# A graph-attention and a graph-convolution layer: q's row through ScalarE's queue, pads in disjoint rows, one full product for the fifth sum, and a new order

## The chip, the cores and the metric

The kernel runs on one core of a Trainium2 chip. The time is the device time of one execution in microseconds (us); several executions are made, and their median is the figure. Everything is computed in float32.

Engines are named as in the profile: PE is TensorE's matmul side, PEld its loading of stationary operands, DVE is VectorE, ACT is ScalarE, POOL is GpSimd and SP is SyncE, which here only issues DMAs. ACT and POOL can issue DMAs too, each on a queue of its own.

## The reference

Two layers work on 32 batches of a 512 x 1024 matrix x (512 channels c, 1024 nodes n). `adj` is 512 x 512, `wq` and `wk` have 512 entries.

```python
# layer 0
h = jnp.maximum(_layernorm(x, axis=-1), 0.0)
q = jnp.einsum('c,bcn->bn', wq, h)
k = jnp.einsum('c,bcn->bn', wk, h)
scores = q[:, None, :] + k[:, :, None]
scores = jnp.where(scores > 0, scores, 0.01 * scores)
att = jax.nn.softmax(scores, axis=-1)
agg = jnp.einsum('bcn,bmn->bcm', h, att)
x = x + jax.nn.relu(jnp.einsum('oc,bcm->bom', adj, agg) + bm[None, :, None])
# layer 1
h = jnp.maximum(_layernorm(x, axis=-1), 0.0)
x = x + jnp.einsum('bnf,nm->bmf', h, adj * adj) + bias
```

The attention of node m depends on q[n] + k[m] alone, with one slope where the sum is positive and another where it is not. The kernel therefore never builds the 1024 x 1024 scores. It sorts the nodes by q, multiplies first (adj times h gives a value vector of 512 for every node), and forms running sums of exp(q) times value from one end of the sorted order and of exp(0.01 q) times value from the other. A node m then needs one row of each sum, picked by the rank of -k[m] among the q.

## The kernel before

For each batch the work is cut into small steps, each a Python function. The names are those of the plan.

- `load` brings the four tiles of x (128 channels x 1024 nodes each, 512 KB). `stats`, `norm`, `slopes` and `relu` make h of them.
- `scores` multiplies h by wq and wk on PE (tile `pq`), copies the result to `qr` on ACT, writes q's 1024 numbers to a DRAM tile `qd` (4 KB) on SP's queue, and reads them back on the same queue, broadcast to 128 partitions, as `qrow` (512 KB). The read waits for the write. `columns` transposes `qr` for q and k by partitions (`qk`). `factors` takes the maximum of q.
- `rank` counts on DVE, for each of 8 blocks of 128 nodes, how many q are smaller. `to_rows` turns four blocks' counts into row indices. `lower` counts on ACT, with Sign, for k; `from_rows` makes indices of that.
- `value` (PE, 8 products of 4 x 128 channels into a PSUM bank each) and `spread` (ACT, PSUM to SBUF) make the value rows; `scatter` writes them on POOL's queue, by index, to their sorted places in a DRAM table `td`. Five tables are used in turn.
- `fetch` reads the sorted table back in three tiles `vs` of three blocks each. There are NB = 9 blocks of 126 nodes, and each block has 2 x 64 rows. All scatters of the batch must have landed. The pool of these tiles has five buffers, so the third tile of a batch waits until sums 3 to 5 of the batch before are through with theirs.
- `weights` takes exponentials of the q column of the fetched rows. `later` adds the identity's columns (`wc`). `stationary` multiplies two 128 x 64 masks by three blocks' weights on POOL (`sm`). `totals` sums the denominators.
- `scan` makes the i-th running sum on PE: two products of 64 columns each, one per direction, for blocks 8 - i and i, into the two halves of one PSUM bank `sc`. `sums` carries the last row of each half into the next blocks (ACT, 1 x 512 copies), copies the bank out and stores it to `td` on SP. So scan i + 1 waits for `sums` i.
- `gather` picks three rows for each node by index on POOL's queue; `excess`, `divide`, `weigh` (ACT) and `combine` (DVE) join them; `turn` transposes on PE and adds to x.
- `reload`, `lift` and the second set of statistics lead to layer 1: `propagate` (PE, 8 pieces of 4 products) and `finish`, which issues the store of the result.

Once, at the start, `adjacency` loads adj, `turn_adjacency` transposes it (16 transposes on PE, four copies on ACT), `square` squares it on POOL, `masks` builds the masks, `biases` loads the bias. `pads` fills the places of the five tables that no node takes: for both directions the first row of every block and all 64 rows of the last block. It issues twenty DMAs from SP.

The order is written out as times. `PLAN` holds a due time for every step, relative to its batch; batch b is moved by b times `T` (80.54). `FIRST` and `LAST` hold a shift and a stretch for the first and last five batches. All steps of all batches are sorted by due time and issued in that order; each engine then runs its own instructions in that order, and waits where data are missing. The times are used for sorting only.

Where two DMAs of SP or ACT share one of eight completion semaphores, the later one also waits for the earlier one.

Of the kernel before, what the change touches and what calls it, by code (L numbers as in the profile page):

```python
# [9 lines left out]
F32 = mybir.dt.float32  # L10
# [6 lines left out]
P = 128  # L17
# [5 lines left out]
QUAD = 32  # L23
# [4 lines left out]
    "adjacency": (-101.07,),  # L28
    "biases": (44.64,),
    "columns": (4.2,),  # L30
    "combine": (
        294.87, 297.97, 299.08, 299.37, 299.3, 299.78, 294.64, 298.25, 297.13,
        300.21, 294.04, 296.69, 302.3, 302.51, 299.3, 302.5,
    ),
    "compare_mask": (-67.81,),
    "divide": (278.8,),
    "excess": (273.86,),
    "factors": (28.62,),
    "fetch": (75.46,),
    "finish": (355.71, 359.91, 377.15, 379.07, 388.37, 416.37, 407.17, 420.62),  # L40
    "from_rows": (83.21,),
    "gather": (249.25, 252.21, 260.07, 256.74, 257.75, 255.56, 251.6, 251.28),
    "later": (83.88,),
    "lift": (346.92, 351.32, 359.81, 351.92),
    "load": (-124.99, -84.4, -100.42, -56.07),
    "lower": (25.57, 12.42, 17.04, 27.8, 11.25, 13.48, 43.56, 47.47),
    "masks": (4.76,),
    "norm0": (-21.98,),
    "norm1": (325.76,),
    "pads": (32.59,),  # L50
    "propagate": (350.28, 351.24, 354.2, 368.59, 377.8, 385.91, 388.55, 393.68),
    "rank": (17.09, 15.7, 21, 21.66, 25, 25.14, 23.99, 25.66),
    "reload": (283.74, 288.13, 272.56, 292.92),
    "relu0": (-11.86, -11.33, -11.17, -11.16),
    "relu1": (334.17, 334.3, 335.44, 339.75),
    "scan": (90.31, 96.47, 108.29, 124.9, 142.06, 153.31, 174.19, 187.88, 206.23),
    "scatter": (46.2, 50.63, 47.64, 43.66, 56.05, 51.39, 52.63, 55.96),
    "scores": (-0.21,),
    "slopes0": (-17.18,),
    "slopes1": (327.63,),  # L60
    "spread": (10.74, 18.48, 13.48, 5.99, 31.17, 24.35, 24.62, 20.5),
    "square": (63.05,),
    "stationary": (83.89, 118.42, 168.32),
    "stats0": (-75.55, -62.59, -67.51, -40.04),
    "stats1": (318.33, 318.56, 319.25, 319.54),
    "sums": (91.26, 100.33, 117.83, 130.05, 147.14, 161.48, 177.9, 193.73, 222.2),
    "to_rows": (25.72, 29.81),
    "totals": (89.77,),
    "turn0": (308.02, 308.31, 307.91, 309.59),
    "turn1": (311.69, 310.85, 311.38, 312),  # L70
    "turn_adjacency": (-8.51,),
    "value": (5.59, 16.27, 4.02, 0.51, 21.28, 16.92, 17.52, 16.87),
    "weigh": (286.06, 287.71, 288.75, 285.95, 287.8, 285.85, 291.87, 291.57),
    "weights": (82.11,),
}
FIRST = {
    "columns": ((11.5, 0), (-7.65, 0), (-3.08, 0), (-4.96, 0), (0.81, 0)),
    "combine": ((11.98, -0.904), (3.93, 0.084), (-0.42, 0.777), (-2.07, 1.063), (3.77, -0.867)),
    "divide": ((-1.51, 0), (4.23, 0), (4.06, 0), (-1.38, 0), (-4.23, 0)),
    "excess": ((2.66, 0), (2.27, 0), (2.29, 0), (3.01, 0), (0.22, 0)),  # L80
    "factors": ((41.36, 0), (40.19, 0), (17.96, 0), (6.13, 0), (12.19, 0)),
    "fetch": ((-6.64, 0), (1.09, 0), (-2.72, 0), (-0.25, 0), (1.04, 0)),
    "finish": ((-0.92, -0.273), (0.38, -0.374), (9.14, 0.111), (-2.55, -0.545), (-1.59, -0.253)),
    "from_rows": ((-13.03, 0), (112.54, 0), (-18.02, 0), (5.07, 0), (43.09, 0)),
    "gather": ((11.61, 0.221), (11.9, -0.839), (7.76, 0.785), (2.8, -0.886), (-0.43, 0.506)),
    "later": ((2.05, 0), (-0.44, 0), (-0.72, 0), (-1.2, 0), (1.78, 0)),
    "lift": ((-3.95, -0.084), (-2.84, -0.648), (17.86, 0.674), (18.88, 0.507), (6.94, 0.337)),
    "load": ((-22.66, 0.032), (-29.56, -0.171), (-16.88, 0.669), (-52.23, 0.939), (-3.3, 0.266)),
    "lower": ((13.95, -0.331), (-5.6, -0.741), (-7.9, -0.46), (7.69, -0.008), (6.58, -0.474)),
    "norm0": ((-17.56, 0), (-16.62, 0), (-4.18, 0), (-1.3, 0), (6.51, 0)),  # L90
    "norm1": ((1.78, 0), (0.29, 0), (-1.09, 0), (0.44, 0), (12.94, 0)),
    "propagate": ((-0.94, -0.576), (-0.21, -0.368), (3.5, -0.199), (5.67, -0.457), (-4.69, -0.221)),
    "rank": ((11.44, 0.484), (9.25, -0.392), (3.13, 1.029), (0.87, -0.157), (3.38, -0.145)),
    "reload": ((-8.27, -0.219), (-0.04, 0.298), (7.54, -0.347), (3.32, -0.281), (9.62, 1.296)),
    "relu0": ((-3.11, -0.86), (0.49, 0.979), (-3.24, 0.727), (-0.45, -0.352), (5.51, -0.464)),
    "relu1": ((2.99, 0.363), (6.63, -0.187), (5.31, -0.95), (8.3, 0.53), (10.39, -0.443)),
    "scan": ((-3.42, -0.009), (-0.72, 0.032), (-3.2, -0.075), (-2.89, -0.005), (-0.35, -0.002)),
    "scatter": ((10.77, 0.257), (-0.73, -0.181), (-11.52, 0.027), (16.18, -0.191), (8.18, 0.362)),
    "scores": ((-3.29, 0), (-9.38, 0), (-3.01, 0), (-4.84, 0), (-2.22, 0)),
    "slopes0": ((-19.05, 0), (4.68, 0), (-8.01, 0), (0.99, 0), (10.12, 0)),  # L100
    "slopes1": ((0.11, 0), (2.69, 0), (11.33, 0), (8.09, 0), (12.97, 0)),
    "spread": ((25.99, 0.616), (4.65, 0.327), (6.4, -0.418), (8.18, -0.066), (2.31, 0.757)),
    "stationary": ((0.59, -0.046), (3.58, 0.024), (-1.58, -0.061), (-4.74, -0.096), (2.23, -0.014)),
    "stats0": ((-18.91, 0.792), (-26.56, 0.18), (-12.87, 0.716), (-14.05, 0.414), (-0.39, 0.587)),
    "stats1": ((1.74, 0.57), (2, -0.774), (-1.08, 0.928), (3.45, -0.808), (5.73, 0.388)),
    "sums": ((-1.76, -0.009), (-1.55, -0.001), (-1.11, -0.098), (-1.11, 0.005), (-0.91, -0.007)),
    "to_rows": ((12.57, 0.861), (6.07, -0.299), (4.35, -0.554), (16.06, 0.147), (-0.33, -0.011)),
    "totals": ((-0.61, 0), (-0.11, 0), (-0.4, 0), (-1.59, 0), (-2.46, 0)),
    "turn0": ((9.6, 0.239), (0.12, 1.463), (3.72, -0.389), (2.48, 1.014), (11.58, 0.097)),
    "turn1": ((5.85, 1.247), (7.03, 0.695), (0.1, -0.107), (-2.36, -0.153), (1.12, 1.09)),  # L110
    "value": ((17.29, 0.126), (-1.93, 0.747), (-1.01, 0.425), (-2.88, 0.246), (-2.48, 0.124)),
    "weigh": ((1.61, 0.137), (0.7, -0.519), (2.4, 0.126), (-4.71, 0.923), (-4.76, -0.192)),
    "weights": ((-3.08, 0), (-0.37, 0), (-0.37, 0), (-1.7, 0), (1.43, 0)),
}
LAST = {
    "columns": ((-7.28, 0), (0.79, 0), (-4.33, 0), (2.89, 0), (0.4, 0)),
    "combine": ((75.93, 0.626), (15.35, -0.941), (5.15, 0.497), (6.86, 0.364), (11.64, -0.543)),
    "divide": ((63.12, 0), (25.51, 0), (3.63, 0), (-8.62, 0), (22.62, 0)),
    "excess": ((28.91, 0), (14.61, 0), (-1.25, 0), (-10, 0), (23.88, 0)),
    "factors": ((-15.6, 0), (18.35, 0), (-16.21, 0), (1.83, 0), (-4.13, 0)),  # L120
    "fetch": ((5.65, 0), (-2.32, 0), (-2.42, 0), (-1.37, 0), (0.79, 0)),
    "finish": ((295.78, -0.788), (84.93, 0.121), (31.35, 0.185), (13.03, 0.342), (8.47, -0.005)),
    "from_rows": ((14.61, 0), (-17.87, 0), (24.1, 0), (-4.82, 0), (-22.08, 0)),
    "gather": ((21.35, -0.228), (-4.99, 0.169), (-6.2, 0.647), (-0.69, 0.387), (24.11, 0.85)),
    "later": ((5.5, 0), (1.61, 0), (-5.88, 0), (-2.68, 0), (0.1, 0)),
    "lift": ((309.49, -0.684), (24.34, 0.156), (8.09, -0.277), (-12.65, 0.02), (0.77, 0.013)),
    "load": ((6.11, 0.011), (-7.3, 0.306), (-3.56, 0.076), (1.31, -0.245), (-2.7, 0.142)),
    "lower": ((25.31, -0.108), (4.14, -0.215), (9.69, -0.156), (2.83, -0.069), (-13.68, -0.57)),
    "norm0": ((-13.5, 0), (-4.32, 0), (-12.1, 0), (0.42, 0), (3.16, 0)),
    "norm1": ((254.22, 0), (9.35, 0), (11.35, 0), (-0.46, 0), (6.61, 0)),  # L130
    "propagate": ((281.75, -0.768), (77.94, 0.675), (26.01, 0.587), (18.85, 0.574), (12.12, 0.012)),
    "rank": ((-6.82, -0.047), (-0.18, 0.987), (3.76, -0.308), (-4.68, -0.157), (-9.98, -0.199)),
    "reload": ((91.8, -0.567), (16.08, -0.302), (4.34, 0.859), (-4.18, 0.357), (-6.61, -0.681)),
    "relu0": ((2.55, -0.699), (0.68, 0.648), (5.21, 0.81), (-0.38, 0.398), (6.21, 0.601)),
# [23 lines left out]
def kernel(  # L158
# [357 lines left out]
    def stationary(s, i):  # L516
# [7 lines left out]
        for n in range(3):  # L524
            s.sm[i + n] = [m[:, k, n, :] for k in range(2)]
# [160 lines left out]
```

## Time and profile before

| | us |
|---|---|
| median of 3 runs | 2416.62 |
| lowest and highest | 2409.54 and 2420.97 |
| profiled execution | 2409.72 |
| span of the profile | 2408.0 |

| engine | busy us | share of the span |
|---|---|---|
| PE | 2307.4 | 96% |
| DVE | 1941.3 | 81% |
| ACT | 1585.4 | 66% |
| POOL | 724.6 | 30% |

The span runs from the first to the last instruction; the execution takes 1.7 us more. The mean granted clock of PE is 0.981 of full speed. An engine's busy time does not say what sets the end: the kernel has a start in which data are missing, a long middle in which every batch looks alike, and an end. They have to be read apart, by stretches of time. In a timeline a row shows the start, the duration, the engine, the line, the operation and its tiles, and in brackets the idle time before it with what ended it. A float32 product appears as two passes, so each PE row counts twice as many instructions as the code has products. The DMA queue of SP appears as SPq, and the time of a DMA there is that of its issue, not of its transfer.

### The profile page before, as it was taken

What the parts mean: (1) busy time and instruction counts of PE and PEld (TensorE: products, weight loads), DVE (VectorE), ACT (ScalarE), POOL (GpSimd) and SP (SyncE); (2) the same over time, 40 slices, a digit from 0 to 9 for tenths busy, and PEclk for the clock granted to TensorE, in tenths of its full rate; (3) what the DMA queues carried; (4) which work ended last, traced back from release to release, by engine and by line L of the source; (5) the groups of instructions that cost most, each with busy time, mean ns of one, the idle gap of its engine ahead of it and who ended that gap; (6) DMA issues with size and microseconds to landing.
All of it is one profiled execution on the core that took longest, in us unless ns stands there. A gap on an engine that the chain in (4) does not pass through costs nothing.

```text
span 2408.0 us, 28425 instructions
## 1 busy us (share of the span) xinstructions
PE 2307.4 (96%) x7632; PEld 1004.8 (42%) x7632; DVE 1941.3 (81%) x5008; ACT 1585.4 (66%) x2880; POOL 724.6 (30%) x973
## 2 busy tenths in 40 slices
PE   6787899999999999999999999999999999999797
PEld 3233344444444444444444444444444444444343
DVE  6448788888888888888888888888898888788675
ACT  4566667667766766777676777676677776677541
POOL 2213332323342232333233233323323313323210
PEclk9898999999999999999999999999999999999899
DMA  4678889988889988988898988898898888888972
GB/s 160 184 184 273 267 264 299 279 265 279 307 262 295 299 262 260 303 290 277 290 285 246 298 295 284 270 309 255 270 304 289 268 294 250 262 268 268 284 290 101
DMA packets 206916, 643.49 MB, mean 267 GB/s; under 512 B 29130, under 2 KB 29258, under 8 KB 206756
## 3 DMA queue, kind: packets, MB, share of 16 engines
q1 hardware_dynamic: 147828, 372.67, 54.1%
q0 software_dynamic: 57344, 268.99, 30.2%
q8 instruction: 62, 1.02, 0.2%
q14 instruction: 98, 0.80, 0.1%
q10 hardware_dynamic: 1584, 0.01, 0.0%
HBM read 429.94 MB, written 211.62 MB: 266 GB/s over the span
## 4 chain that ended last, share of the span: by engine, by line
PE 86%; DMA 6%; DVE 3%; ACT 2%; issue 1%; SPq 1%; POOL 1%; POOLq 0%; DVEq 0%; ACTq 0%
PE pg L595 34%; PE pv L447 33%; PE sc L530 12%; PE tr L588 4%; DMA vs<-td 3%; PE pq L344 2%; DVE g L581 1%; DMA td<-pad 1%; DMA g<-td,idg 1%; DVE junk L389 0%; DMA out_dram<-y 0%; DMA x<-in_x_dram 0%; ACT junk L400 0%; DMA qd<-qr 0%; POOL g L552 0%
## 5 line engine op out<-in xcount | busy, mean ns | idle before, releaser
L595 PE MATMUL pg<-h,wsq 128*128 128x512 f32 x2048 | 912.7, 598 | 11.1 <-ACT h L332 11.1
L447 PE MATMUL pv<-wmT,x 128*128 128x512 f32 x2048 | 909.5, 599 | 5.6 <-ACT x L332 5.6
L595 PEld LDWEIGHTS pg<-h,wsq 128*128 128x128 f32 x2048 | 378.7, 190 | 510.0 <-issue 468.5
L447 PEld LDWEIGHTS pv<-wmT,x 128*128 128x128 f32 x2048 | 383.3, 191 | 498.7 <-issue 439.3
L520 POOL TENSOR_TENSOR sm<-mask_a,wc 128x192 f32<-128x192 f32 x96 | 49.9, 519 | 1289.4 <-DVE wc L497 830.9
L530 PE MATMUL sc<-vs,sm 128*64 128x512 f32 x1152 | 324.2, 631 | 60.0 <-POOL sm L520 39.2
L581 DVE SCALAR_TENSOR_TENSOR g<-g,cf 128x512 f32<-128x512 f32 x512 | 347.8, 746 | 12.4 <-ACT g L577 12.4
L460 POOL DMA_INDIRECT td<-v,idx x256 | 293.7, 1147 | 148.8 <-POOL v L459 50.7
L400 ACT ACTIVATE junk<-qrow,qk 128x1024 bf16<-128x1024 f32 x256 | 294.3, 1150 | 4.9 <-DMA qrow<-qd 3.1
L552 POOL DMA_INDIRECT g<-td,idg x256 | 242.9, 949 | 143.6 <-issue 71.6
L540 ACT COPY vs<-sc 1x512 f32<-1x512 f32 x256 | 145.4, 568 | 171.3 <-PE sc L530 171.1
L590 DVE SCALAR_TENSOR_TENSOR y<-tr,nbm,y 128x512 f32<-128x512 f32 x256 | 174.2, 743 | 95.4 <-PE tr L588 89.1
L543 ACT COPY t<-sc 128x512 f32<-128x512 f32 x288 | 168.0, 583 | 94.4 <-DMA td<-t 89.4
L603 DVE SCALAR_TENSOR_TENSOR y<-pg,bm_sb,y 128x512 f32<-128x512 f32 x256 | 187.9, 738 | 42.6 <-PE pg L595 42.3
L389 DVE TENSOR_SCALAR_CACHE_REDUCE junk<-qrow,qk,cnt 128x896 bf16<-128x896 f32 (+6 forms) x224 | 180.4, 805 | 8.2
L530 PEld LDWEIGHTS sc<-vs,sm 128*64 128x64 f32 x1152 | 77.8, 139 | 253.6 <-issue 91.3
L314 DVE BATCH_NORM_STATS2 st<-x 128x6 f32<-128x512 f32 x256 | 162.9, 678 | 25.0 <-DMA x<-in_x_dram 25.0
L384 DVE TENSOR_SCALAR_CACHE_REDUCE junk<-qrow,qk 128x128 bf16<-128x128 f32 (+6 forms) x224 | 165.5, 739 | 13.6 <-DMA qrow<-qd 8.8
L577 ACT ACTIVATE g<-g,cf 128x512 f32<-128x512 f32 x256 | 163.5, 711 | 7.4 <-DVE cf L571 7.4
L338 DVE TENSOR_TENSOR y<-y,bias_sb 128x1024 f32<-128x1024 f32 x128 | 155.1, 1230 | 8.4 <-ACT h L332 8.4
L314 DVE BATCH_NORM_STATS2 st<-y 128x6 f32<-128x512 f32 x256 | 159.1, 663 | 0.0
L454 ACT COPY v<-pv 128x512 f32<-128x512 f32 x256 | 142.2, 580 | 21.6 <-PE pv L447 17.8
(109 smaller groups left out, 1939.0 us busy)
## 6 DMA issues: line engine op xcount, KB each, us to landing
vs<-td SPq DMA_DIRECT2D x192, 384.8 KB
td<-t SPq DMA_DIRECT2D x576, 128.2 KB
x<-in_x_dram SPq DMA_DIRECT2D x128, 512.0 KB
y<-in_x_dram SPq DMA_DIRECT2D x128, 512.0 KB
out_dram<-y SPq DMA_DIRECT2D x128, 512.0 KB
qrow<-qd SPq DMA_DIRECT2D x32, 512.0 KB
td<-v,idx POOLq DMA_INDIRECT x256, 7.6
g<-td,idg POOLq DMA_INDIRECT x256, 11.0
```

Of the source, the lines that this page charges most:

```text
L314: nc.vector.bn_stats(st[:, i, :], s.x[c][:, ts(i, HALF)])
L389: nc.vector.tensor_scalar(junk[:, j * P :], s.qrow[:, j * P :], qc, first, ALU.is_lt, ALU.add, accum_out=s.cnt[:, 1, j : j + 1],)
L400: nc.scalar.activation(junk, s.qrow, AF.Sign, bias=s.qk[:, 1, j : j + 1], accum_out=s.sgn[:, j : j + 1])
L447: nc.tensor.matmul(pv, s.h[c][:, ts(j, P)], wmT[:, c, :], start=(c == 0), stop=(c == NC - 1))
L460: i = nc.gpsimd.indirect_dma_start(tds[s.b % TABLES][:, :], bass.IndirectOffsetOnAxis(ap=s.idx[j // 4][:, j % 4 : j % 4 + 1], axis=0), v[: ...
L530: nc.tensor.matmul(p[ts(k, HP), :], s.sm[i][k], s.vs[h][:, 0:C], start=True, stop=True)
L543: nc.scalar.copy(t[:, 0:C], p)
L552: nc.gpsimd.indirect_dma_start(s.g[:, j, :], None, tds[s.b % TABLES][0 : 3 * NB * HP, :].rearrange("(s k) w -> s (k w)", k=3), bass.Indire ...
L581: nc.vector.scalar_tensor_tensor(r, s.g[:, j, k * W : k * W + C], s.cf[:, k, j : j + 1], r, ALU.mult, ALU.add)
L590: nc.vector.scalar_tensor_tensor(xh, pt, nbm[:, o : o + 1], xh, ALU.max, ALU.add)
L595: nc.tensor.matmul(pg, wsq[:, r, ts(c, P)], s.h[r][:, ts(i, HALF)], start=(r == 0), stop=(r == NC - 1),)
L603: nc.vector.scalar_tensor_tensor(xh, s.pg.pop((c, i)), bm_sb[:, c : c + 1], xh, ALU.add, ALU.add)
```

## The change

Four things are changed.

1. `scores` still issues the write of q to DRAM, but on ACT's queue. The read of `qrow` becomes a step of its own, `row`, with its own due time, also on ACT's queue.
2. `pads` writes the first row of the first NB - 1 blocks and all rows of the last block. The two stores no longer share a row.
3. `stationary` lays its result out so that the two 64-column halves of a block lie side by side. In the fifth sum (i = 4) both directions work on the same block; there `scan` makes one product of 128 columns in place of two of 64.
4. All times in `PLAN`, `FIRST` and `LAST` are new, and `T` is 80.4.

```diff
@@ pads
-                nc.sync.dma_start(sorted_rows(td, 0, NB)[o, 0], pad[0:NB, :])
+                nc.sync.dma_start(sorted_rows(td, 0, NB - 1)[o, 0], pad[0 : NB - 1, :])
                 nc.sync.dma_start(sorted_rows(td, NB - 1, 1)[o, :, 0], pad[0:HP, :])
@@ scores
         nc.scalar.copy(s.qr, pq)
-        qd = qds[s.b % 2]
-        nc.sync.dma_start(qd, s.qr[0:P:QUAD, :])
+        nc.scalar.dma_start(qds[s.b % 2], s.qr[0:P:QUAD, :])
+
+    def row(s):
         s.qrow = wp.tile([P, N], F32, tag="qrow", name=f"qrow_{s.b}")
-        nc.sync.dma_start(s.qrow, qd.rearrange("g n -> (g n)").partition_broadcast(P))
+        qd = qds[s.b % 2].rearrange("g n -> (g n)")
+        nc.scalar.dma_start(s.qrow, qd.partition_broadcast(P))
@@ stationary
-        m = sp.tile([P, 2, 3, HP], F32, tag="sm", name=f"sm_{s.b}_{i}")
+        m = sp.tile([P, 3, 2, HP], F32, tag="sm", name=f"sm_{s.b}_{i}")
...
-                m[:, k], mask.unsqueeze(1).broadcast_to([P, 3, HP]),
+                m[:, :, k, :], mask.unsqueeze(1).broadcast_to([P, 3, HP]),
...
-            s.sm[i + n] = [m[:, k, n, :] for k in range(2)]
+            s.sm[i + n] = m[:, n]
@@ scan
         p = bank(f"sc_{s.b}_{i}")
-        for k, h in enumerate((NB - 1 - i, i)):
-            nc.tensor.matmul(
-                p[ts(k, HP), :], s.sm[i][k], s.vs[h][:, 0:C], start=True, stop=True
-            )
-        s.sm.pop(i)
+        m = s.sm.pop(i)
+        ha, hb = NB - 1 - i, i
+        if ha == hb:
+            both = m.rearrange("p k r -> p (k r)")
+            nc.tensor.matmul(p, both, s.vs[ha][:, 0:C], start=True, stop=True)
+        else:
+            for k, h in enumerate((ha, hb)):
+                nc.tensor.matmul(
+                    p[ts(k, HP), :], m[:, k, :], s.vs[h][:, 0:C], start=True, stop=True
+                )
         s.pt[i] = p
@@ the due times, as far as the prediction speaks of them
 PLAN = {
...
-    "pads": (32.59,),
+    "pads": (1.15,),
...
+    "row": (1.98,),
...
-    "scores": (-0.21,),
+    "scores": (-1.83,),
...
-    "square": (63.05,),
+    "square": (53.38,),
...
-    "turn_adjacency": (-8.51,),
+    "turn_adjacency": (-39.9,),
...
-    "value": (5.59, 16.27, 4.02, 0.51, 21.28, 16.92, 17.52, 16.87),
+    "value": (3.89, 14.52, -1.07, 4.1, 20.69, 18.74, 15.77, 15.86),
...
 FIRST = {
...
-    "load": ((-22.66, 0.032), (-29.56, -0.171), (-16.88, 0.669), (-52.23, 0.939), (-3.3, 0.266)),
+    "load": ((-114.53, -0.719), (-41.9, -0.581), (-61.5, -0.134), (-67.36, 0.974), (-10.03, 0.381)),
...
+    "row": ((-2.93, 0), (-19.24, 0), (-8.82, 0), (3.92, 0), (-1.39, 0)),
...
-    "scores": ((-3.29, 0), (-9.38, 0), (-3.01, 0), (-4.84, 0), (-2.22, 0)),
+    "scores": ((-48.13, 0), (-16.76, 0), (-5.07, 0), (-5.89, 0), (-6.97, 0)),
...
-    T = 80.54
+    T = 80.4
```

In the order that follows, the fourth tile of the first batch's x is loaded ahead of the adjacency (it was behind it); the first scores come ahead of the adjacency's transposes on PE (they were behind); `pads` comes ahead of the ranks on DVE and behind ten loads of x on SP; `square` comes ahead of the first scatters on POOL (it was between the fifth and the sixth). In the second batch four values come ahead of the first scan of the first batch (there were three). From batch 5 on `row` stands behind `weights` on ACT in nearly every batch, while `scores` stands ahead of them. Between the fifth scan of a batch and the first of the next PE has the scores and three values in both.

## The prediction

> **What bounds the kernel now.** I read the page first (busy shares, then the 40 slices), then the busy time by stretches of 75 us, then the chain, TensorE's and SyncE's timelines of the stretches that are not full, and last what SyncE's queue waits for.
>
> ```profile
> PE 2307.4 (96%) x7632; PEld 1004.8 (42%) x7632; DVE 1941.3 (81%) x5008; ACT 1585.4 (66%) x2880; POOL 724.6 (30%) x973
> 0.00:75.00 75.00, 50.19 (x172) 22.27 (x172) 43.57 (x135) 29.26 (x45) 15.18 (x29) 0.94 0.57 176
> 75.00:150.00 75.00, 62.09 (x188) 25.11 (x189) 42.71 (x142) 52.97 (x105) 17.33 (x32) 0.88 0.62 164
> 150.00:225.00 75.00, 55.72 (x168) 20.35 (x167) 47.02 (x155) 51.41 (x105) 28.32 (x41) 0.83 0.89 264
> 225.00:300.00 75.00, 68.16 (x223) 30.93 (x221) 56.00 (x147) 48.90 (x88) 22.04 (x33) 0.94 0.82 250
> 1125.00:1200.00 75.00, 75.00 (x252) 32.25 (x251) 63.87 (x173) 52.81 (x95) 22.51 (x31) 1.00 0.88 281
> 2175.00:2250.00 75.00, 62.41 (x187) 26.66 (x187) 58.07 (x140) 47.58 (x89) 29.57 (x38) 0.94 0.92 281
> ```
>
> In the stretches the first pair after the length is PE, then PEld, DVE, ACT, POOL, granted clock, DMA share, GB/s. From about 330 to 2,020 us TensorE has no gap worth naming at clock 1.00; a batch returns every 70.93 us (the chain):
>
> ```profile
> 541.86 17.36 PE pv L447 x40
> 612.79 17.36 PE pv L447 x40
> ```
>
> 32 batches of 70.93 are 2,269.8 us. The span, 2,408.0, is 138 more. Gaps of PE, summed from its timeline, are 35.8 us up to 115 us, 29.1 from there to 325, and 35.1 from 2,028 to the end; the other 38 are the transposes of the adjacency (3.6) and work at a lower clock behind gaps (0.83 to 0.94 above). So two things can shorten this kernel: less work on PE in each batch, or a fuller start and end.
>
> The start is held by SyncE's queue:
>
> ```profile
> 34.23 0.31 SPq L267 DMA_DIRECT2D td<-pad  x1
> 35.78 0.50 SPq L268 DMA_DIRECT2D td<-pad  x1
> 62.32 0.45 SPq L268 DMA_DIRECT2D td<-pad  x1
> 62.81 1.07 SPq L301 DMA_DIRECT2D x<-in_x_dram  x2
> 65.15 3.96 SPq L477 DMA_DIRECT2D vs<-td  x6
> 69.83 0.55 SPq L351 DMA_DIRECT2D qd<-qr  x1
> 81.58 0.33 SPq L353 DMA_DIRECT2D qrow<-qd  x1
> ```
> ```profile
> 82.75 2.43 PE L530 MATMUL sc<-vs,sm 128*64 128x512 f32 x4 [13.71 <-POOL sm L520]
> ```
> ```profile
> SPq L353 <- DMA qd<-qr: 177.6, 32, 11.1
> SPq L268 <- DMA td<-pad: 18.1, 10, 3.1
> ```
>
> The 20 pad stores hold the queue from 34.23 to 62.77, since every second one waits for the one before it: the 9-row store and the 64-row store both write the first row of the last block. Behind them stand three loads of x, the bias and the first fetch (65.15), whose last third lands at 81.5; PE waits 13.71 us for it (through w, wc and sm). Behind the fetch stands q's 4 KB write of the second batch: issued 69.83, landed 81.58.
>
> **The change part by part.**
>
> *Pads.* The rows are disjoint, so the ten waits (18.1 us) go. The order on SP also moves: the pads come after the tenth load of x and ahead of three others, the memset on DVE ahead of the ranks. Of the twenty stores, the eighth shares a DMA semaphore with the first q row, so SP stands there till that lands (about 26); twelve more at some 0.55 us end near 33. All four x loads follow at once (2 MB, in 6 us at the 380 GB/s of the first 16 us) and are off the queue long before the fetch. The first table's four pads are in before that wait, so they no longer hold the first scatter (issued at 41.52 though its ranks stood at 39.5).
>
> *First batch.* x[3] is now ahead of the 1 MB adjacency: its stats, which waited 2.64 us for it, come some 2.7 us earlier, so the row's write goes out near 18.7 (was 21.96). But the transposes (3.59) now follow the scores on PE instead of filling its wait for x, and the row's second DMA stands on ACT behind their four copies (2.01). So it goes out near 22.3 (was 23.66) and lands at 26.3: 1.3 us gained of 3.2. Value products start where they did (22.4) and end near 51.3. Ranks: five of 1.7 to 2.0 us and to_rows 1.45 give the first indices at 37.7; the second half at 45.3. `square` (3.61), which cut the scatters at 48.9, moves ahead of them. The last scatter then waits for the last spread alone: issued near 52.5 (was 55.9), landed near 57. SP is free, so the fetch goes out at 57.3 against 65.15. From issue to last landing it took 16.3 us with 2 MB of other data ahead, and the next two fetches 13.9 and 13.8; I take 14: 71.3. Then w, wc, sm (1.3): first scan at 73, was 82.75: **9.75 us**. If the fetch runs in an empty system (2.36 MB at 380 GB/s, 4 us of issuing, 2 of latency) it is 68; if it keeps its 16.3, 75.5.
>
> *After the first scan.* PE has four values of batch 1 behind it then, not three, and so only four to do before batch 2's: some 27 us where 31.1 passed (82.75 to 113.84). Batch 1's ranks start as soon as den is copied (75) since the row is there; their second indices come near 95.4, were 105.4; last scatter 101, fetch 105.5 (was 115.32), first scan of batch 1 near 120.4 (was 130.26). PE waits some 8 us there (was 1.84), so the extra lead is given back, and the chain's 10 us remain. From there both orders are alike until batch 3: there the indices are ordered ahead of `excess`, which waits for the gather (they stood behind it, 201.7 to 210.7), and the fifth scan behind the transposes of batch 0. The fetch waited for scatters that landed at 232.5; now the third tile alone waits for that scan. I expect most of the 6.84 us gap before 249.52 to go: 5 us. Sum for the start: **15 us**, ends 6 and 24.
>
> *Fifth sum.* Alone between products of 128 columns, its pair holds PE for 1.01 us, two in a row for 0.935 each; a full product holds it for 0.868:
>
> ```profile
> 1126.89 1.94 PE L530 MATMUL sc<-vs,sm 128*64 128x512 f32 x8
> 1148.18 1.08 PE L530 MATMUL sc<-vs,sm 128*64 128x512 f32 x4
> 1149.19 3.70 PE L595 MATMUL pg<-h,wsq 128*128 128x512 f32 x8
> ```
>
> (Start to start: 1,148.18 to 1,149.19 for x4; x40 of full passes last 17.36, two passes to a product.) Saved: 0.14, times 32, **4.5 us**. The Trainium skill, "TensorEngine Tiling (Array Packing)", section Theoretical Speedup, gives a product of 64 columns up to twice the rate when two run in independent tiles. By it the pair would already cost what one full product costs, and the edit would save nothing. The row is 16% above that, so I take the row; ends 0 and 6.5 (with 0.07 us for the switch of shape on either side). Work on GpSimd for the masks is the same four products per pair of tiles (519 ns each) in another layout; it ends at 1,175.04 where PE needs it at 1,177.04, so a slower one by 0.5 each would be hidden just.
>
> *Row on ACT's queue.* Two DMA issues per batch move from SP (0.54 and 0.33) to ACT: 28 us of 822 that ACT sits idle. In the steady stretch the write stands ahead of `weights`, which wait 1.79 us for the fetch anyhow; the row stands behind them in nearly every batch, 5.7 us after the write. What the write takes on ACT's queue no row shows: 1.68 us is the nearest in an empty system (21.96 to 23.66), 11.75 the longest on SP behind a fetch. The Trainium skill, "DMA: Bandwidth & Descriptors", section Rules for kernel authors, says that spreading DMAs over queues only saves issue time, all running on the same 16 engines. By it the fetch and the row would be as late as before and I should strike the row's share; its section Queues, rings and completion order says that an engine takes packets in turn from the rows it serves, and then four packets need not queue behind 2.4 MB. I take 3 us. In the steady stretch nothing comes of it: ranks are not what PE waits for. It matters in batch 1, where 11.75 becomes 3, and is in the 10 us above. If it does not, batch 1's row comes with the fetch, near 71, and the ranks still start near 76: 1 us lost.
>
> *New times.* Values start with tile 2, transposes and pieces of the second product swap places; PE's work between fifth scan and first scan of the next batch (one score, three values, 12.6 us) is the same, so the steady cover is the same. At the end the fetch of the last batch still stands behind the sixth scan with three pieces of product (10.4 us) as cover, so the 12.59 us gap stays; the last gap (11.09, from transposes to relu) stays, with one piece less between the last two sets of transposes (38 us for 37 that the chain needs). I take 0, ends -6 and +6.
>
> **Sum.** 15 + 4.5 + 0 = 19.5 us. The profiled execution took 2,409.7 (span 2,408.0 and 1.7 around it): 2,390 against it. That execution is 6.9 below the median of the runs shown, 2,416.6; against the median, 2,397. The forecast is 2,396.
>
> **The rivals.** *The start gives its lead back* (0.14): chain and PE meet again at a later wait, say the 18 us lost between 204 and 226 where ACT interleaves sums with weigh and lower, which the change leaves in kind. Then 4.5 of sums and 0 to 6 of start: 2,406 to 2,412. For it: PE's gaps from 115 to 325 are no fewer in the order. Against: they hang on the chain that starts earlier.
>
> *More goes* (0.12): the fetch in 11 us and the gaps of 204 to 250 closed by the new order: 30 to 36 us, 2,380 to 2,387.
>
> *ACT stands at the row* (0.04, slower). The row waits on ACT for the write. Till 9.0 us after its issue this is hidden (5.7 of other work and 3.29 idle before the copy at 1,178.22). From there PE's second scan is late by every microsecond: at the 11.1 that SP waited at most, 2.1 us in each of some 27 batches, 57 us, less the 19.5: about 2,454. Against it: SP's mean wait was 5.5 (177.6 over 32).
>
> **How the numbers follow.** Main case 0.70: 15 (6 to 24) and 4.5 (0 to 6.5), the end ±6: 2,384 to 2,408, nearly all under 2,404.5, which is 0.5% below the median and about what a measurement can tell from none. With the rivals: faster 0.82, within 0.5% 0.14, slower 0.04. Range 2,380 to 2,410.
>
> **What would show it.** Right: pads off SP before 35; first fetch issued near 57 and first scan near 73; PE's gaps before 325 down from 65 to about 50; period 70.8 and sc of 1,088 products, 64 of 128 columns. Wrong: a first scan later than 80, new gaps of PE from 330 on, ACT idle before the row's DMA beyond 3 us per batch, a gap above 15 us after 2,200, or a period of 71 or more.

## The result, and the profile after

| kernel | median us | lowest to highest | ratio to before, 95% interval |
|---|---|---|---|
| before | 2415.42 | 2409.54 to 2420.97 | |
| after | 2385.51 | 2384.92 to 2390.79 | 0.9881, 0.9854 to 0.9909 |
| after, a second set | 2389.11 (before: 2412.29) | 2383.67 to 2391.91 | 0.9900, 0.9885 to 0.9915 |

The first row has one run more than the section on the kernel before. The changed kernel is 1.0 to 1.2% faster: 23 to 30 us, where 20 were forecast. The two profiled executions differ by less, 2,408.0 against 2,389.1 us of span: that of before is the fastest of its set, that of after the slowest of its. So the spans below account for 18.9 us.

First the pads. SyncE's queue, from its timeline (start, duration of the issue, queue, line, transfer):

```profile
24.04 0.35 SPq L272 DMA_DIRECT2D td<-pad  x1
...
29.59 1.77 SPq L273 DMA_DIRECT2D td<-pad  x1
...
34.99 0.45 SPq L273 DMA_DIRECT2D td<-pad  x1
...
54.92 4.10 SPq L484 DMA_DIRECT2D vs<-td  x6
```

Twenty stores pass in 11.4 us, with one stop of 1.3 us (the 1.77), where 28.5 were needed before. From 38.3, when the bias's load is out, to 54.92 nothing stands ahead of the fetch in the queue; the fetch now waits for the scatters, the last of which POOL issued at 49.38. q's row, on ACT's queue, and what PE then gets:

```profile
55.53 0.51 ACTq L355 DMA_DIRECT2D qd<-qr  x1
59.77 0.34 ACTq L360 DMA_DIRECT2D qrow<-qd  x1
```
```profile
70.56 0.38 PE L516 MATMUL pd<-w,mask_a 128*64 128x9 f32 x2 [4.79 <-ACT w L493]
71.47 2.43 PE L543 MATMUL sc<-vs,sm 128*64 128x512 f32 x4
120.37 6.55 PE L543 MATMUL sc<-vs,sm 128*64 128x512 f32 x16
234.24 1.11 PE L543 MATMUL sc<-vs,sm 128*64 128x512 f32 x3 [2.64 <-POOL sm L527]
308.63 0.38 PE L516 MATMUL pd<-w,mask_a 128*64 128x9 f32 x2 [2.77 <-ACT w L493]
311.21 0.28 PE L517 MATMUL pd<-e,ones 128*64 128x9 f32 x1 [2.20 <-DVE e L508]
```

And before, batch 3's first scan; then the block of 40 value passes behind batch 4's first sums, before and after:

```profile
249.52 4.14 PE L530 MATMUL sc<-vs,sm 128*64 128x512 f32 x8 [6.84 <-POOL sm L520]
328.93 17.36 PE pv L447 x40
316.35 17.36 PE pv L454 x40
```

The first scan is 11.3 us earlier than before. PE waited 13.71 us just ahead of it; now it waits 4.79, ahead of the totals, and then little. Batch 3's first scan, the last one that the forecast timed, stands at 234.24 for 249.52: 15.3 us, and the gap ahead of it is 2.64 for 6.84. Then two gaps (308.63 and 311.21, 5.0 together where before had 0.9) give some back, and the block of 40 value passes that follows is 12.6 ahead. The busy time by stretches (length, then PE, PEld, DVE, ACT and POOL with their instructions, granted clock, DMA share, GB/s) says the same:

```profile
0.00:75.00 75.00, 54.62 (x194) 24.00 (x195) 43.58 (x148) 33.47 (x56) 17.45 (x34) 0.96 0.73 213
75.00:150.00 75.00, 64.23 (x184) 24.47 (x182) 45.96 (x158) 55.55 (x109) 21.63 (x38) 0.93 0.61 154
150.00:225.00 75.00, 58.62 (x221) 24.64 (x222) 51.66 (x144) 51.34 (x99) 23.24 (x32) 0.89 0.93 271
225.00:300.00 75.00, 72.36 (x239) 32.09 (x238) 60.02 (x156) 48.65 (x90) 25.67 (x32) 1.00 0.87 265
```

PE is busy 249.8 us of the first 300, before 236.2, and at a higher clock in each of the four. Now the period, from the chain:

```profile
743.27 17.36 PE pv L454 x40
813.80 17.36 PE pv L454 x40
```

70.53 us for 70.93. The fifth sum is a form of its own in the groups (stationary and moving operand, count, then busy us and mean ns of one, then idle time before):

```profile
L543 PE MATMUL sc<-vs,sm 128*64 128x512 f32 x1024 | 287.5, 629 | 12.5 <-ACT vs L552 4.9 <-POOL sm L527 3.5 <-DVE den L521 1.6
L540 PE MATMUL sc<-vs,sm 128*128 128x512 f32 x64 | 34.7, 625 | 11.7 <-ACT vs L553 11.7
```

1,024 and 64 passes instead of 1,152. Last the end of the run, before and after: two gaps where before had 12.59, and the one ahead of the last product.

```profile
2249.19 4.27 PE L530 MATMUL sc<-vs,sm 128*64 128x512 f32 x7 [12.59 <-POOL sm L520]
2374.03 29.21 PE L595 MATMUL pg<-h,wsq 128*128 128x512 f32 x64 [11.09 <-ACT h L332]
```
```profile
2226.82 0.38 PE L516 MATMUL pd<-w,mask_a 128*64 128x9 f32 x2 [7.53 <-ACT w L493]
2233.75 4.91 PE L543 MATMUL sc<-vs,sm 128*64 128x512 f32 x12 [2.25 <-ACT vs L552]
...
2353.73 30.59 PE L607 MATMUL pg<-h,wsq 128*128 128x512 f32 x64 [10.67 <-ACT h L337]
```

The 18.9 us of span add up by blocks of 40 value passes, which both traces have: 12.6 at 316.35; 4.5 between there and 1,802.13 (before 328.93 to 1,819.19), less than 21 batches at 0.40, since one stretch (457.86 to 531.46) took 73.6; -1.2 to 2,094.14 (before 2,110.02); 3.0 from there to the end. By idle time of PE: 54.9 us before 330 us (before 64.9), 5.5 from there to 2,000 (before 0.5) and 25.0 behind that (before 30.4), 10.4 less in all; the rest is less work, 2,298.7 us of busy PE for 2,307.4. So the changed kernel also has 5 us of new gaps in the middle, near 515 to 527 and 1,893 to 1,944. The kernel with all the code under the old times (`code_only`, below) has 0.2 us there, so they come with the new order.

### The profile page after: what moved, and what is told of

It is laid out like the page before. It is cut to its first block, busy times and chain, and to the rows that moved or that the text cites. A ratio compares the mean times of both kernels' runs of the same rounds, so it can differ in the third digit from the quotient of the medians.

```text
span 2389.1 us, 28172 instructions
## 1 busy us (share of the span) xinstructions
PE 2298.7 (96%) x7568; PEld 1016.2 (43%) x7568; DVE 1957.4 (82%) x5008; ACT 1589.4 (67%) x2878; POOL 719.5 (30%) x973
## 4 chain that ended last, share of the span: by engine, by line
PE 84%; DMA 7%; DVE 4%; ACT 3%; issue 1%; SPq 1%; POOL 0%; ACTq 0%; DVEq 0%; POOLq 0%
PE pg L607 35%; PE pv L454 31%; PE sc L543 10%; PE tr L600 4%; DMA vs<-td 3%; PE pq L349 2%; DMA td<-t 2%; PE sc L540 1%; DVE g L593 1%; DVE st L319 1%; DMA qd<-qr 1%; DVE junk L396 1%; DMA wqk<-in_L_gnn_wk_dram 1%; DMA g<-td,idg 1%; SPq L484 0%
## 5 line engine op out<-in xcount | busy, mean ns | idle before, releaser
L527 POOL TENSOR_TENSOR sm<-mask_a,wc 128x192 f32<-128x192 f32 x96 | 57.3, 596 | 1128.5 <-DVE wc L504 718.8
L593 DVE SCALAR_TENSOR_TENSOR g<-g,cf 128x512 f32<-128x512 f32 x512 | 363.2, 777 | 6.4 <-ACT g L589 3.6
L467 POOL DMA_INDIRECT td<-v,idx x256 | 285.1, 1114 | 251.7 <-POOL v L466 41.4
L543 PE MATMUL sc<-vs,sm 128*64 128x512 f32 x1024 | 287.5, 629 | 12.5 <-ACT vs L552 4.9
L337 ACT ACTIVATE x<-x,nmr,rstd 128x1024 f32<-128x1024 f32 x128 | 148.8, 1231 | 38.4 <-DVE nmr L330 38.4
```

The lines of the kernel that those rows point to most:

```text
L467: i = nc.gpsimd.indirect_dma_start(tds[s.b % TABLES][:, :], bass.IndirectOffsetOnAxis(ap=s.idx[j // 4][:, j % 4 : j % 4 + 1], axis=0), v[: ...
L543: nc.tensor.matmul(p[ts(k, HP), :], m[:, k, :], s.vs[h][:, 0:C], start=True, stop=True)
L593: nc.vector.scalar_tensor_tensor(r, s.g[:, j, k * W : k * W + C], s.cf[:, k, j : j + 1], r, ALU.mult, ALU.add)
```

## Experiments

The theory to be tested: the start gains from the pads' ten waits; the period gains from the one product; the row on ACT's queue and the new times bring nothing themselves. Rivals: the new order brings part of the period; the row is what lets the new order work; ACT stands still at the row.

### Each part alone, and all code under the old times

`pads_alone` and `sum_alone` are the kernel before with one edit; `times_only` has the new `PLAN`, `FIRST`, `LAST` and `T` and the old code; `code_only` has all three edits of the code, the old times, and one time for the new step:

```diff
     "relu1": (334.17, 334.3, 335.44, 339.75),
+    "row": (1.6,),
```

Expected of `pads_alone`:

> The kernel before with only the rows of the pads made disjoint. My theory (the ten waits on SyncE's queue hold the first fetch): the pads end near 45 instead of 62.8, the three loads of x and the bias near 47, the first fetch goes out when the last scatter has landed, near 60.5 instead of 65.15, and lands in 14 us: first scan near 76 instead of 82.75. The second batch's fetch hangs on its own ranks and gains less; the time falls by 3 to 7 us. Rival (the pads only move the wait, since the row of q of the second batch still stands behind the fetch): first scan near 76, but the second batch's first scan stays within 2 us of 130.26 and the time within 2 us of before. The period of the middle stays 70.93 by both.

Of `sum_alone`:

> The kernel before with only the full product for the fifth sum (and the layout that it needs). The kernel after repeats every 70.53 us where before took 70.93. My theory after seeing that: the product saves 0.15 in itself and 0.10 because TensorE no longer changes its shape before and behind it, 0.25 together; the rest is the order. So the period here is 70.68 and the time falls by 8 us. Rival (the product alone, as forecast): 0.14, period 70.79, 4.5 us. Second rival (all of it is the product): 70.53, 13 us.

Of `code_only`:

> All three edits of the code with the old times; the row's step, which the old times lack, is put behind weights on ScalarE (1.6, no shifts). Theory: period 70.68 as with the product alone; first scan near 76 as with the pads alone; 11 to 15 us faster than before. Rival (the new order carries the start, the edits nothing without it): first scan within 3 us of 82.75, only the 8 us of the period.

Of `times_only`:

> The old code with the new times: pads overlap, the row is written and read on SyncE's queue at the time of scores, two products for the fifth sum. Theory: period 70.78 (the order's 0.15); the pads begin near 24 and with their waits end near 53, before the scatters have landed, so the first fetch is hardly later than in the kernel after and the first scan near 72 to 76; the second batch's row stands behind the fetch, which costs that batch's first scan 2 to 4 us (122 to 125). Total 12 to 18 us faster than before. Rival (the edits carry the start): first scan beyond 78, second batch beyond 127.

Measured, in one set with before at 2,413.88:

| kernel | median us | ratio, 95% interval | first scan of batch 0 | period |
|---|---|---|---|---|
| pads_alone | 2405.40 | 0.9958, 0.9941 to 0.9974 | 74.66 | 70.93 |
| sum_alone | 2408.78 | 0.9973, 0.9962 to 0.9984 | 82.42 | 70.59 |
| code_only | 2396.06 | 0.9931, 0.9914 to 0.9947 | 74.22 | 70.53 |
| times_only | 2444.68 | 1.0122, 1.0095 to 1.0149 | 84.33 | 70.93 to 71.06 |

The pads alone move the first scan by 8.1 us, batch 1's first scan by 7.0 (123.26 for 130.26, so the rival of `pads_alone` fell), and leave the period. The sum alone leaves the first scan and moves the period by 0.34. Together the two ratios would give 0.9931, and that is what all the code has under the old times: the row on ACT's queue adds nothing there that these intervals, some 6 us to either side, could show. The share of the period that the new order was thought to bring fell: under the new times alone the period is not below 70.93.

The periods show a small share of the queue. They fall into pairs: 70.93 and 70.59 with the row on SyncE's queue, two products and one, and 70.87 (`pair_back`, below) and 70.53 with it on ACT's; `queue_back`, which differs from the changed kernel in the queue alone, has 70.58. So of the 0.40 the product has 0.34, and 0.06 goes with the queue, 2 us in 32 batches. It sits in the three sums behind the totals, 3.43 us from start to start in `sum_alone` and 3.36 in the changed kernel:

```profile
1175.74 3.49 PE L536 MATMUL sc<-vs,sm 128*64 128x512 f32 x12
1092.57 3.44 PE L543 MATMUL sc<-vs,sm 128*64 128x512 f32 x12
```

What delays these sums when the row is on SyncE's queue is not shown.

`times_only` is the surprise: 31 us slower than before. Its SyncE queue and PE:

```profile
59.90 0.53 SPq L356 DMA_DIRECT2D qd<-qr  x1
66.21 0.33 SPq L358 DMA_DIRECT2D qrow<-qd  x1
...
67.34 4.10 SPq L482 DMA_DIRECT2D vs<-td  x6
```
```profile
83.42 0.39 PE L514 MATMUL pd<-w,mask_a 128*64 128x9 f32 x2 [13.45 <-ACT w L491]
```

In the new order q's write of the second batch stands ahead of the first fetch, and with the old code SyncE waits for it (59.90 to 66.21) before it can issue that fetch. Ahead of the totals PE has gaps near the end too, 7.70 at 1,908.78 and 8.50 at 2,141.91, where before has none of that size till 2,249. Two parts of the old code could be the cause, the pads' waits and the row on SP, so each was put back alone.

### Each part put back

`pair_back`, `queue_back` and `pads_back` are the changed kernel with one edit undone. Of the first:

```diff
-        if ha == hb:
-            both = m.rearrange("p k r -> p (k r)")
-            nc.tensor.matmul(p, both, s.vs[ha][:, 0:C], start=True, stop=True)
-        else:
-            for k, h in enumerate((ha, hb)):
...
+        for k, h in enumerate((NB - 1 - i, i)):
```

> The changed kernel with one part undone: the fifth sum is two products of 64 columns again, in the new layout of the masks. Theory A (the product is the whole of the period's gain, as the run with the sum alone had it: 70.59 against 70.93): period 70.87, 32 x 0.34 = 11 us slower than the changed kernel, about 2,396, ratio to the kernel before 0.992. Theory B (my prediction's size, 0.14 a batch, the rest from the new order of the transposes): period 70.67, about 2,390. First scan stays at 71.5 in both.

Measured: 2,395.98, ratio 0.9923 (0.9897 to 0.9949), as theory A had it. Its first scan is at 68.78, not near 71.5: in six executions with the start of the changed kernel it lies between 68.8 and 72.4, so 2 us there are not a difference. This kernel has the order of the changed one, so a period can be read row by row against it. PE's timeline of the changed kernel, around the fifth sum:

```profile
1055.04 2.03 PE L543 MATMUL sc<-vs,sm 128*64 128x512 f32 x8
1057.00 7.13 PE L607 MATMUL pg<-h,wsq 128*128 128x512 f32 x16
1063.97 1.02 PE L540 MATMUL sc<-vs,sm 128*128 128x512 f32 x2
1064.83 7.03 PE L607 MATMUL pg<-h,wsq 128*128 128x512 f32 x16
```

And with the pair back:

```profile
1061.67 2.02 PE L538 MATMUL sc<-vs,sm 128*64 128x512 f32 x8
1063.63 7.13 PE L602 MATMUL pg<-h,wsq 128*128 128x512 f32 x16
1070.69 1.08 PE L538 MATMUL sc<-vs,sm 128*64 128x512 f32 x4
1071.70 7.13 PE L602 MATMUL pg<-h,wsq 128*128 128x512 f32 x16
```

From start to start: the piece of product ahead of the pair holds PE for 7.06 us, ahead of the full product for 6.97; the pair for 1.01, the full product for 0.86; the piece behind it (to the transposes at 1,078.67 and 1,071.70) for 6.97 and 6.87. That is 0.09 + 0.15 + 0.10 = 0.34 us, which is the difference of the periods: 70.87 (the blocks of 40 value passes at 961.14 and 1,032.01) against 70.53. So the change between products of 64 and of 128 columns goes with some 0.1 us each way, and it shows in the rows of the neighbours. The kernel before has it too. There eight passes hold PE for 3.54 us behind a pair (1,149.19 to 1,152.73), and for 3.43 between two sets of transposes, which use all 128 columns:

```profile
1152.73 0.60 PE L588 MATMUL tr<-ident,g 128*128 128x128 f32 x4
1153.17 3.60 PE L595 MATMUL pg<-h,wsq 128*128 128x512 f32 x8
1156.60 3.22 PE L588 MATMUL tr<-ident,g 128*128 128x128 f32 x28
```

The Trainium skill, "TensorEngine Tiling (Array Packing)", section Key Properties, says that a change of tiling mode drains TensorE. It gives no time for it; these rows agree with it and give one, though that the 0.1 us are a drain is the page's word and not seen in a row.

The row back on SyncE's queue:

```diff
-        nc.scalar.dma_start(qds[s.b % 2], s.qr[0:P:QUAD, :])
+        nc.sync.dma_start(qds[s.b % 2], s.qr[0:P:QUAD, :])
...
-        nc.scalar.dma_start(s.qrow, qd.partition_broadcast(P))
+        nc.sync.dma_start(s.qrow, qd.partition_broadcast(P))
```

> The changed kernel with both of q's transfers on SyncE's queue again, the row still a step of its own at its new place. Theory A (the new times need ACT's queue: the old code under these times lost 30 us to late fetches): SyncE stands at the row till the write lands, behind the fetch of the batch before, and the next fetch and loads stand behind that; new gaps of PE ahead of w in the steady part, 2,400 to 2,430. Theory B (only the second batch's row matters, 1 us lost, as the prediction had it): 2,386 to 2,388. First scan of batch 0 within 2 us of 71.5 in both, second scan later than 120.4 by over 5 us in A.

Measured: 2,417.14, ratio 1.0012 (1.0004 to 1.0020). The size is theory A's: under the new times the queue is worth as much as the whole change. But A had the loss in the steady part, and there the period is 70.58. It is lost among the first and the last batches. Nor did the first scan stay within 2 us of 71.5. SyncE's queue at the start and near 450 us:

```profile
56.94 0.54 SPq L355 DMA_DIRECT2D qd<-qr  x1
58.62 0.33 SPq L360 DMA_DIRECT2D qrow<-qd  x1
...
59.73 4.04 SPq L484 DMA_DIRECT2D vs<-td  x6
...
453.02 0.52 SPq L355 DMA_DIRECT2D qd<-qr  x1
466.65 0.33 SPq L360 DMA_DIRECT2D qrow<-qd  x1
```

The first fetch is 4.8 us later than in the changed kernel (54.92), the first scan 4.9 (76.35). The blocks of 40 value passes are 8.0 us later at 324.32, 14.7 at 546.15, 15.0 at 1,817.13, 20.2 at 2,043.81, and 27.1 at 2,121.27, of which 25.6 are left at the end. What stands in the queue behind a row that waits for its write is late, sums' stores and loads among them (13.6 us from the write to the row at 453.02). In the prediction the rule that spreading DMAs over queues saves issue time only (the Trainium skill, "DMA: Bandwidth & Descriptors", section Rules for kernel authors) stood against this part of the change. Issue time is 0.85 us a batch; what the runs show is a wait taken off a queue that other work must pass, worth 28 to 32 us under one order and within 6 us of nothing under another.

The overlapping pads back:

```diff
-                nc.sync.dma_start(sorted_rows(td, 0, NB - 1)[o, 0], pad[0 : NB - 1, :])
+                nc.sync.dma_start(sorted_rows(td, 0, NB)[o, 0], pad[0:NB, :])
```

> The changed kernel with the overlapping pad stores back, so that every second store waits for the one before. Theory A (the start term is the pads' waits): ten waits of some 1.8 us end the pads near 50 instead of 35; the first fetch goes out some 7 us later, first scan near 78, and 4 to 7 us of that remain at the end: 2,390 to 2,393. Theory B (the pads now start 10 us earlier than before and are off the queue before the last scatter needs it): first scan stays at 71.5 to 73, time 2,385 to 2,387. Period 70.53 in both.

Measured: 2,393.76, ratio 0.9926 (0.9911 to 0.9941), 5 to 8 us more than the changed kernel, as theory A had it:

```profile
53.22 0.45 SPq L273 DMA_DIRECT2D td<-pad  x1
...
60.29 6.87 SPq L484 DMA_DIRECT2D vs<-td  x6
```

The last pad leaves at 53.22 instead of 34.99, the fetch at 60.29 instead of 54.92, and the first scan at 77.19 is 5.7 us later. The block of value passes that was at 316.35 is at 322.08: the lead of the start is kept to there.

Undone one at a time, the three edits cost 0.016 to 0.022 of the time of before (each ratio less that of the changed kernel, 0.9881 or 0.9900). Undone together, in `times_only` (where the row is no step of its own either), they cost 0.022 to 0.024. So the three account for most of what the new times lose without the edits; whether all of it, these intervals do not tell.

### The slower rival: ACT stands at the row

Only the times of the row differ from the changed kernel: in batches 5 to 26 the read of the row is ordered directly behind the write.

```diff
-    "row": (1.98,),
+    "row": (-1.82,),
```

(The shifts of the first and last five batches take the 3.8 back.)

> The changed kernel with the row directly behind the write of q on ACT's queue in batches 5 to 26 (22 batches), the other batches at their places. ACT then stands still for the whole of the write. Theory A (the write takes 3 to 5 us on this queue, and ACT has 3.9 us of idle time ahead of weights to give): ACT waits some 4 us a batch for the write, and weights no longer wait; time 2,384 to 2,389. Theory B (my slower rival: the write stands behind the fetch as on SyncE's queue and takes up to 11 us): ACT waits about 11, PE's second scan is late by 2 to 3 us in each of 22 batches: 2,430 to 2,450.

Measured: 2,394.18, ratio 0.9913 (0.9885 to 0.9941), 5 to 9 us above the changed kernel. Neither number holds. ACT's waits for the write (us in total, times, longest):

```profile
ACT w L491 <- DMA qd<-qr: 146.1, 23, 8.5
```

ACT stands idle for 6.35 us at the mean, with the issue of both DMAs in it. From the issue of the write to that of the row it is 5.9 us at the mean of the 22 batches and 8.1 at the longest, not the 3 to 5 of theory A nor the 11 of B. The rival's point of decision was 9.0, and no batch reached it. From 609.68 to 1,742.60 a period is 70.81 at the mean of 16, in the changed kernel 70.60 (601.99 to 1,731.61): 0.2 us a batch, some 5 over the 22. It is not lost where the rival had it: the three sums behind the totals, the second scan among them, hold PE for 3.37 us as in the changed kernel. It is lost at the two sums ahead of the sixteen passes that precede the fifth sum. The worst batch, and one of the changed kernel:

```profile
780.66 2.54 PE L543 MATMUL sc<-vs,sm 128*64 128x512 f32 x8
772.93 1.94 PE L543 MATMUL sc<-vs,sm 128*64 128x512 f32 x8
```

There ACT's copy of a carry starts 0.20 us after the pair in the first (780.86) and 0.47 ahead of it in the second (772.46). So the wait costs some time, by the look of the rows through what ACT does later, and the row's step of its own, behind the weights, keeps it out of the steady part of the changed kernel.

### What the new times are worth, and the end

The first set gave 10 us between `code_only` and the changed kernel, but from two sets of runs. Both were run again together, with a kernel that fills the gap ahead of the last product:

```diff
+            if name in ("propagate", "finish") and s.b == B - 2 and n > 4:
+                t += 300
+            if name == "combine" and s.b == B - 1:
+                t -= 13
             steps.append((t, len(steps), f, (s, *lead, *(args[n] if args else (n,)))))
```

In this kernel, `tail`, the additions of `combine` come ahead of `weigh` for blocks 1, 3 and 7 of the last batch, so those blocks are scaled after the addition instead of before. That is no longer the same sum, so `tail` stands here for its times alone.

> The changed kernel once more, beside the next two, so that small differences are read within one set of runs. Both theories: 2,385 to 2,391, ratio to the kernel before about 0.989.

> All three edits of the code under the old times, the row behind the weights on ACT's queue, once more beside the changed kernel. Theory A (the new times are worth some 10 us on top of the code): 2,395 to 2,398, ratio to before 0.993. Theory B (the 10 us came from comparing two sets of runs, since the two profiled executions differ by 1 us only): within 3 us of the changed kernel.

> The changed kernel with the last three pieces of the second product of batch 30 (three times 3.5 us of PE) moved behind the last transposes of batch 31, and batch 31's combines 13 earlier in the order, so that PE has work in the last gap (10.67 us before the last product). Theory A (the gap is waiting for the chain of batch 31 from transposes to relu, which then starts earlier by up to three pieces): the last gap falls to some 1 us and 5 to 9 us go: 2,377 to 2,381. Theory B (the combines on DVE set when the last transposes can run, so that the moved pieces only leave a gap ahead of them): the gap moves there, 2,384 to 2,392.

Measured, with before at 2,412.29: the changed kernel 2,389.11 (0.9900, 0.9885 to 0.9915), the code under old times 2,392.41 (0.9922, 0.9906 to 0.9938), `tail` 2,388.85 (0.9891, 0.9873 to 0.9909). The new times on top of the code are worth 3 us here and 10 between the first sets; the intervals overlap, and their size stays open. The two profiles of this set differ most at one place: the code under old times has a gap of 18.01 ahead of 2,231.23, the changed kernel 1.56 and 4.19 ahead of 2,220.93 and 2,227.86. (In the first profile of the changed kernel they were 7.53 and 2.25: this wait differs between executions.) At the start the block of 40 value passes, 7.0 us ahead with the pads alone, is 10.5 and 11.2 ahead with all the code under old times, and 12.6 and 11.7 in the changed kernel.

`tail` went by theory B. PE at its end:

```profile
2334.74 0.33 PE L600 MATMUL tr<-ident,g 128*128 128x128 f32 x1 [1.18 <-DVE g L593]
2336.73 0.33 PE L600 MATMUL tr<-ident,g 128*128 128x128 f32 x1 [1.66 <-DVE g L593]
2342.02 0.47 PE L600 MATMUL tr<-ident,g 128*128 128x128 f32 x1 [4.96 <-DVE g L593]
...
2360.56 28.56 PE L607 MATMUL pg<-h,wsq 128*128 128x512 f32 x64 [2.96 <-ACT h L337]
```

The last gap falls from 10.68 (the changed kernel in this set) to 2.96, and 7.8 us of waits for the combines appear ahead of the transposes: 10.8 in all. One more run left the combines where they were and moved only the three pieces and their finishes:

> The changed kernel with the last three pieces of the second product of batch 30 and their finishes moved behind the last transposes of batch 31; nothing else moves. In the changed kernel's second profile the last transposes start at 2,334.51, 1.5 us after the last combine, and four finishes of 0.75 us stand among the combines. Theory A (the chain gather, divide, combine, transposes sets the end, and the moved finishes free DVE): transposes some 2.6 us earlier, a gap of 7 to 8 us ahead of them, the last gap down from 10.68 to some 1 us, the time 2 to 3 us less than the changed kernel's 2,389, ratio to before 0.989. Theory B (the combines wait for the weighing on ACT, not for DVE): transposes at the same distance, no gain, ratio 0.990.

Measured: 2,395.99 with before at 2,420.47, ratio 0.9902 (0.9884 to 0.9920). In the profile the last product follows without a gap, and 7.9 us of waits remain ahead of the transposes: 2.8 of 10.68 are gone. From the arrival of the last gather to the end of the span the changed kernel took 66.6 us (2,316.80 to 2,383.4), this one 64.0 (2,341.49 to 2,405.5). That is theory A's size, but the ratio does not show it; in this profile a wait of 17.00 ahead of the last totals, for the last fetch, is far larger. No version measured beats the changed kernel by more than the intervals can tell.

## Why the prediction was right, and where it was off

The sign held, and with it the pads as the first cause and the product as the second. The gain of 23 to 30 us is 3 to 9 more than the 20 forecast. In the profiles the total, 18.9 for 19.5, is nearer than its parts, and that is luck: the start brought 12.6 for 15 and the middle new gaps of 5 us for none, while the product brought more than was counted.

- *Pads and first batch.* Pads off the queue near 33, measured 35.4; they waited for their memset on DVE till 24.04, which the working left out. First fetch at 57.3, measured 54.92, since the last scatter went out at 49.38 and not 52.5; from its issue to the last weights' start it took 15.3 and not 14. So two errors cancel in part in the first scan: 73 forecast, measured 71.47. Second scan at 120.4, measured 120.37; in the other executions with this start it lies between 116.4 and 121.9, so that nearness is luck too. The working took 380 GB/s for the first 16 us; the trace has 299 there, and 373 from 5 to 12. Nothing hung on it.
- *Start term, 15 us.* 15.3 at batch 3's first scan, 12.6 behind batch 4's. `pads_alone` had 7.0 of it there (321.94 for 328.93), and `pads_back` lost 5.7. Idle time of PE before 330 fell from 64.9 to 54.9, not to 50: the two gaps at 308 and 311 gave 2.7 back, which no step had.
- *Fifth sum, 4.5 us.* This is the step that was mis-sized. The term counted the pair's own 0.14 us, and left the switch of shape on either side to the upper end, at 0.07 in all. The rows showed 0.15, 0.09 and 0.10: 0.34 a batch, 7 us in the 21 batches of the steady part, and 11 if all 32 gain alike. Undoing it cost 7 to 10 us (`pair_back`); alone it brought 5 by the medians and 4 to 9 by its interval, since it gains little where PE waits anyhow. The rows of before that say so were there: ahead of the fifth sum sixteen passes held PE for 7.06 us (1,141.12 to 1,148.18), behind it eight for 3.54 (1,149.19 to 1,152.73), where at 0.434 each, as in the blocks of 40, they take 6.94 and 3.47.
- *Row on ACT's queue.* The write was taken at 3 us; it took 4.2 in batch 1 and, with the row directly behind, 5.9 in the steady part. Its share was put at 1 us, and at nothing in the steady part, where it is 0.06 a batch. Under the new times it is 28 to 32, since the prediction asked only what is late when the row is late, and not what stands behind it on SyncE's queue in the new order.
- *New times, 0, ends -6 and +6.* On top of the code 3 to 10 us were gained; without the code 31 are lost. As a sum of parts the prediction was right by treating the times as one with the edits; as a statement on the times alone it was not.
- *The end.* It was to stay. The 12.59 became 7.53 and 2.25, the 11.09 became 10.67.
- *Signs of being wrong.* One came in small: new gaps of PE from 330 on, 5 us in all. No other came: the first scan is at 71.5 and the largest gap behind 2,200 is 10.67.
- *Rivals.* The start kept its lead. "More goes" had the total of the first set, but not its reasons: the fetch took 15.3 us and not 11, and the gaps of 204 to 250 closed only in part. ACT does not stand at the row in the steady part of the changed kernel; it does in four of the first and last batches, for 4.7 to 8.0 us, and in one of these the weights are late by it and PE waits 2.1 us (1,944.28). By `row_at_once`, standing there in every batch would not have cost 57 us.

## What to carry to other kernels

A change of shape between products is priced from start to start over the neighbours too, not from the row that changes. A DMA that waits for another one is costed by what is queued behind it, and that depends on the order: the same move was worth too little to measure under one list of times and 28 us or more under another. So an edit and its order are measured together, and each is also undone from the whole. A gap at the end is only filled with the engine that ends the wait in view: moving PE's work there moved the gap to DVE's combines.

## What was not expected of the hardware

- The 4 KB write is not faster on ACT's queue. From its issue to that of the row directly behind it, batches 5 to 26 took 5.9 us at the mean and 8.1 at the longest there (`row_at_once`), and 6.1 and 9.7 on SyncE's queue in the kernel before. What the other queue changes is who waits. It was not shown whether the write waits for packets of the fetch or for other traffic.
- The mask products on POOL in the new layout take 596 ns for 519 (mean of 96, `mask_a`), and 574 for 561 (`mask_b`), though the work is the same. Nothing waited for the difference in the steady part.
